# Attention weights sent through DRAM: each softmax row stored twice, copied from there to the partitions of its head, and the output projections spread over the step

## The chip, the cores and the metric

The kernel runs on one NeuronCore of one Trainium2 chip. It is one program that holds four layers one after the other, all in float32. The time is the device time of one execution in microseconds. The kernel before was timed three times: 10415.69 us is the median, 10412.58 the lowest and 10416.83 the highest. One further execution was recorded by the hardware profiler; it has its own time, given with its span below.

The engines are named as in the profile: PE is TensorE (matrix products), PEld its weight loads, DVE is VectorE, ACT is ScalarE, POOL is GpSimd, and SP is SyncE, which here only issues DMA transfers. Each engine runs its own instructions strictly in order and waits for others by semaphores.

## The reference, cut to what matters

The input x has 8 images, 16 channels, 128 x 128 points. Four layers are applied, each as x = x + layer(groupnorm(x)). Only the first one is touched in its inner loop:

```python
def layer0(in_x, w_attn, w_attn_proj, w_fc, w_fc_proj, conv_w, conv_b):
    # per point: the 3x3 neighbourhood, wrapped, as 3 tokens of 48 (a column of 3 rows x 16 channels)
    x = fold(in_x)                                  # [N, 3, 48],  N = 8*128*128
    h = ln(x)
    q, k, v = split(h @ w_attn.T)                   # 4 heads of 12
    att = softmax(einsum('nhtd,nhsd->nhts', q, k) / sqrt(12))      # 3 x 3 weights per head
    y = einsum('nhts,nhsd->nhtd', att, v)
    x = x + y @ w_attn_proj.T
    h = ln(x)
    x = x + gelu(h @ w_fc.T) @ w_fc_proj.T          # 48 -> 192 -> 48
    x = ln(x)
    return conv1x1(sum(x, axis=tokens)) + conv_b
```

The three tokens s of a query t are the left, middle and right neighbours, and since the weights add to one, y = v_middle + a_left (v_left - v_middle) + a_right (v_right - v_middle). Both kernels use this: they need only two of the three weights, and the differences dv of neighbouring v.

## The kernel before, in words

**Tiling.** Layer 0 (lines 242 to 786) goes over the image in 32 steps of 4 rows, that is 512 points of each image. A tile has 128 partitions: two images (g), each with 48 values of a token in a block of 64 partitions, and 512 points in the free dimension. Eight images make four such pairs k; d = 0, 1 counts couples of pairs, so that a tile of 128 x 1024 holds two pairs. PSUM has 8 banks of 512 columns, `banks`: bank 0 collects variances, bank 1 the attention scores, and the rest is handed out in pairs of banks by `two()`, in a ring.

**A software pipeline.** The loop at line 688 runs four stages of four successive steps side by side. `ahead` (two steps on) is loaded and centred (`load`, `center`); `then` (one step on) gets its first normalization, q, k, v, the products q*k (`multiply`), the scores (`scores`) and the softmax; `new` gets attention, projection, second normalization and the first four of its six MLP units; `old` gets the last two units (4 and 5), the variances for the last normalization, and the final sum; `done` is stored.

**Order.** Matrix products are emitted in the order of the program and held in it by `in_turn("pe", ...)` (lines 218 and 374). So the PE has one fixed list, and a product that waits for its input holds up all that follows it. The attention products on DVE and POOL are held in turn in the same manner. The lists of the other engines come from the program's order and the scheduler, and are in order too.

**The attention step before.** `softmax` (line 510) leaves normalized weights `att` on 96 partitions: row 32*u + 8*k + 4*g + h for the query u, the pair k, the image g and the head h. The values v have one partition per head element, so each weight row must be copied to the 12 partitions of its head. `attend(k, j, at)` (line 533) does this with three matrix products by a 0/1 matrix `spread` into three PSUM banks; DVE multiplies those with `dv` into `y` (line 543, 128 x 1536, one operand in PSUM), and POOL subtracts it from v or adds it (lines 551 and 553, 128 x 1536). There are 8 such calls in a step: four pairs k, and j = 0 (left), 2 (right). `project` (line 556) multiplies y by the projection `wpc`, and DVE adds the result to the centred input (line 565).

**Where they stand.** The part that follows the softmax is a list of 8 slots, `between` (lines 696 to 741). Each slot begins with one `attend` and then has pieces of other work: units 4 and 5 of `old` in slots 0 to 5, back projections and projections 0,0 to 0,2 in slots 6 and 7, and then `qkv` of the next step. Projections 1,0 to 1,2 stand behind the slots, line 744.

**Queues.** SP issues the loads of `xin` (24 a step), the load and store of the finished rows (lines 619 and 627) and, in step 0, the small weights of layer 1 (line 734). ACT issues the other constants at the start. In layer 1, ACT issues the loads `bs` (line 845) ahead of its square root.

Of the kernel before, what the change touches and what calls it, by code (L numbers as in the profile page):

```python
# [9 lines left out]
F32 = mybir.dt.float32  # L10
AF = mybir.ActivationFunctionType
ALU = mybir.AluOpType
# [24 lines left out]
def _constants():  # L37
# [20 lines left out]
    score[token, 24 + 4 * g + h] = 1.0  # L58
    parts["score"] = score
    spread = np.zeros((128, 4, 128))  # L60
    bcast = np.zeros((128, 5, 128))
    last = np.zeros((128, 2, 2, 32))
    for t in range(4):
        bcast[32 * t + 16 + g, 4, token] = 1.0
        for n in range(4):
            bcast[32 * t + 4 * (n // 2) + 2 * (n % 2) + g, n, token] = 1.0
            spread[32 * t + 8 * n + 4 * g + h, n, token] = 1.0
# [3 lines left out]
    parts["spread"] = spread.reshape(128, 512)  # L71
# [34 lines left out]
def kernel(  # L106
# [29 lines left out]
    from_ = _WHERE["pair"][1]  # L136
    const = cpool.tile([128, _CONST.shape[1] - from_], F32, name="const")
    nc.scalar.dma_start(const, const_in[:, from_:])

    def k_(name):  # L140
        n, lo, hi = _WHERE[name]
        return const[:n, lo - from_ : hi - from_]
# [83 lines left out]
    w1s, b1s = [], []  # L226
    for n in range(5):
        t = cpool.tile([BC, BC], F32, name=f"w1_{n}")
        nc.gpsimd.memset(t, 0.0)
        for b in range(B):  # L230
            r = slice(b * C, (b + 1) * C)
            loads.append((t[r, r], w1[n].rearrange("i o -> o i") if n < 2 else w1[n]))
        w1s.append(t)
        b1s.append(rep(b1[n], B, f"b1_{n}"))
# [7 lines left out]
    with ExitStack() as l0:  # L242
# [19 lines left out]
        def k0(name):  # L262
# [4 lines left out]
        spread, bcast = (  # L267
            k0(name).rearrange("p (n m) -> p n m", m=128) for name in ("spread", "bcast")
        )
# [27 lines left out]
        for i in range(3):  # L297
            for g in range(2):
                r = slice(64 * g + i * 16, 64 * g + i * 16 + 16)
                nc.scalar.dma_start(  # L300
                    wqkv[r, :, :E], w0_qkv[i].rearrange("c (n o) -> c n o", n=3)
                )
# [13 lines left out]
        for g in range(2):  # L316
            nc.scalar.dma_start(wpc[64 * g : 64 * g + E, :E], w0_proj)
# [39 lines left out]
        def work(name):  # L357
            return tmp.tile([128, 2, 512], F32, tag="work", name=name, bufs=11)

        def large(name):  # L360
            return tmp.tile([128, 3, 512], F32, tag="large", name=name, bufs=5)
# [56 lines left out]
        class Step:  # L418
# [23 lines left out]
            def center(self, d):  # L442
                p = two()
                blocks(p, lambda k: wcen[:, 2 * d + k], xin[:, 2 * d : 2 * d + 2])
                self.xc[d] = act.tile([128, 2, 512], F32, name="xc", bufs=5)
# [17 lines left out]
            def qkv(self, d):  # L463
                q = self.q[d] = work("q")
# [19 lines left out]
            def multiply(self, d, engine):  # L484

                for k in range(2):
                    parts = []
                    for at, n in ((0, 3), (3, 2)):
                        t = large("pd")
                        ins = (nc.vector if engine == "dve" else nc.gpsimd).tensor_mul(  # L490
                            t[:, :n].rearrange("p n (a b) -> p n a b", a=4),
# [18 lines left out]
            def softmax(self):  # L510

                a = self.att = act.tile([96, 3, 512], F32, name="att")
# [1036 lines left out]
```

## Time and profile before

| what | value |
|---|---|
| median of 3 runs | 10415.69 us |
| time of the profiled execution | 10417.28 us |
| its span, first to last instruction | 10415.5 us |
| layer 0, from the span's start | about 0 to 3192 us |
| one steady step of layer 0 | 94.45 us (the same product starts at 1509.06 and 1603.51 us) |
| busy in 1000 to 2000 us | PE 913, DVE 507, ACT 548, POOL 639 us |
| DMA share in the same stretch | 6% of 16 engines, 15 GB/s |

Busy shares are averages over the four layers; layers 2 and 3 take the time after about 3320 us and are bound by other engines than layer 0. What a change in layer 0 is worth is read from one steady step: which engine works without a gap, and what ends its gaps. In timeline rows the columns are start (us), length (us), engine, line, operation, what is written and read, and in brackets the idle time before it and what ended it. A product in float32 shows as two matmul records. The granted clock of TensorE (PEclk) is a share of full speed.

### The profile page before, as it was taken

Reading aid. Unit: us, or ns where it says so; the run is one execution under the profiler, and the core shown is the slowest. Engines: PE = TensorE matmul, PEld = TensorE weight load, DVE = VectorE, ACT = ScalarE, POOL = GpSimd, SP = SyncE. Lnnn points to the kernel's source line nnn. Section 1 sums busy time; section 2 is a strip of 40 time slices with the busy share of each in tenths; the row PEclk is TensorE's granted clock in tenths of the full one; section 3 lists DMA queues with packets and bytes.
Section 4 is the critical chain, followed back from the end, with each engine's and each line's share of the span. In section 5 each row is a group of like instructions: output and inputs, shape, how many; then the busy total and the mean of one; then the engine's idle time right before and its main releaser. Section 6 shows DMA issues by size and latency. Waiting matters only on the chain.

```text
span 10415.5 us, 192029 instructions
## 1 busy us (share of the span) xinstructions
PE 8808.0 (85%) x81400; PEld 2482.8 (24%) x81400; DVE 8490.1 (82%) x6774; ACT 8595.5 (83%) x7107; POOL 5545.7 (53%) x2608
## 2 busy tenths in 40 slices
PE   6999999999996888888888888888888888888799
PEld 1222222222222222222222222222222222222222
DVE  4545554554555999999999999999999999999977
ACT  3555555555555999999999999999999999999988
POOL 4666666666652555555555555555555555555421
PEclk8999999999998999999999999999999999999999
DMA  1000000000002000000000000000000000000022
GB/s 53 13 15 15 14 14 15 15 13 15 15 7 77 14 21 16 18 21 14 21 14 21 14 20 21 14 21 14 21 14 21 17 18 20 14 13 9 14 62 62
DMA packets 203668, 215.74 MB, mean 21 GB/s; under 512 B 50616, under 2 KB 159416, under 8 KB 200760
## 3 DMA queue, kind: packets, MB, share of 16 engines
q1 hardware_dynamic: 197544, 198.27, 7.0%
q8 instruction: 640, 10.49, 0.4%
q10 hardware_dynamic: 5264, 5.17, 0.2%
q14 instruction: 220, 1.80, 0.1%
HBM read 117.80 MB, written 60.04 MB: 17 GB/s over the span
## 4 chain that ended last, share of the span: by engine, by line
DVE 43%; PE 25%; issue 21%; ACT 8%; DMA 2%; SPq 1%; POOL 0%; DVEq 0%; ACTq 0%; POOLq 0%
PE banks L375 18%; DVE u L1078 15%; DVE pn L1078 10%; DVE u L1082 9%; DVE t L1068 2%; PE pn L1019 2%; PE pd L1019 2%; PE acc L1398 2%; DVE y L543 2%; DVE x L565 1%; ACT hid L157 1%; ACT sq L571 1%; ACT u L157 1%; DMA f<-yd 1%; DVE x L662 1%
## 5 line engine op out<-in xcount | busy, mean ns | idle before, releaser
L1091 POOL TENSOR_TENSOR v<-t,u 128x1280 f32<-128x1280 f32 x1152 | 3449.8, 2995 | 3080.8 <-DVE t L1068 3044.7
L1068 DVE SCALAR_TENSOR_TENSOR t<-t,u 128x2048 f32<-128x2048 f32 x1152 | 2632.7, 2285 | 32.3 <-ACT u L157 31.2
L1019 PE MATMUL pd<-f,wb 32*64 32x512 f32 x18432 | 2510.2, 608 | 92.8 <-ACT t L1057 40.5
L1057 ACT ACTIVATE t<-pd 128x1024 f32<-128x1024 f32 x2304 | 2364.9, 1026 | 133.2 <-PE pd L1019 75.0
L1019 PE MATMUL pn<-f,wa 32*64 32x512 f32 x18432 | 1299.4, 615 | 1112.1 <-DVE u L1082 1111.9
L157 ACT ACTIVATE u<-u 128x2048 f32<-128x2048 f32 x1152 | 2208.9, 1917 | 0.0
L157 ACT ACTIVATE u<-t 128x2048 f32<-128x2048 f32 x1152 | 2204.0, 1913 | 0.0
L1078 DVE TENSOR_TENSOR u<-pn,u 128x1280 f32<-128x1280 f32 x1152 | 1718.8, 1492 | 122.2 <-DVE pn L1078 2.8
L157 ACT ACTIVATE hid<-banks 128x1024 f32<-128x1024 f32 x576 | 569.9, 1023 | 1049.6 <-PE banks L375 1048.3
L1110 PE MATMUL acc<-u,const 128*32 128x512 f32 (+2 forms) x13824 | 1112.1, 454 | 0.0
L1078 DVE TENSOR_TENSOR pn<-pn,u 128x768 f32<-128x768 f32 x1152 | 1103.3, 958 | 0.0
L1082 DVE SCALAR_TENSOR_TENSOR u<-t,pn 128x768 f32<-128x768 f32 x1152 | 1087.6, 944 | 0.0
L1019 PEld LDWEIGHTS pd<-f,wb 32*64 32x64 f32 x18432 | 615.1, 130 | 1249.6 <-ACT t L1057 891.8
L1019 PEld LDWEIGHTS pn<-f,wa 32*64 32x64 f32 x18432 | 275.7, 130 | 2117.2 <-DVE u L1082 2109.7
L1110 PE MATMUL acc<-v,const 128*32 128x512 f32 (+1 forms) x9216 | 763.2, 449 | 1.5 <-POOL v L1091 1.5
L490 POOL TENSOR_TENSOR pd<-q,kp 128x1536 f32<-128x1536 f32 x248 | 674.6, 2732 | 11.2 <-PE banks L375 9.1
L571 ACT ACTIVATE sq<-x 128x1024 f32<-128x1024 f32 x384 | 395.3, 1053 | 272.6 <-DVE x L565 172.8
L375 PE MATMUL banks<-h,wfc 64*128 64x512 f32 (+1 forms) x3072 | 598.5, 617 | 14.6 <-DVE h L638 14.6
L638 DVE TENSOR_TENSOR h<-banks,x 128x1024 f32<-128x1024 f32 x192 | 232.6, 1211 | 428.2 <-PE banks L375 219.2
L543 DVE TENSOR_TENSOR y<-banks,dv 128x1536 f32<-128x1536 f32 x256 | 448.2, 1751 | 140.4 <-PE banks L375 134.1
L1110 PEld LDWEIGHTS acc<-u,const 128*32 128x32 f32 x13824 | 366.6, 109 | 812.6 <-issue 812.6
L553 POOL TENSOR_TENSOR y<-y 128x1536 f32<-128x1536 f32 x128 | 442.1, 3454 | 197.8 <-DVE y L543 197.5
(198 smaller groups left out, 8370.6 us busy)
## 6 DMA issues: line engine op xcount, KB each, us to landing
f<-yd SPq DMA_DIRECT2D x1016, 60.9 KB
yd<-y SPq DMA_DIRECT2D x280, 130.0 KB
xin<-in_x SPq DMA_DIRECT2D x744, 32.0 KB
four<-sil SPq DMA_DIRECT2D x256, 65.0 KB
xj<-in_x SPq DMA_DIRECT2D x8, 1024.0 KB
s<-in_x SPq DMA_DIRECT2D x32, 256.0 KB
x1d<-s SPq DMA_DIRECT2D x32, 256.0 KB
x<-x1d SPq DMA_DIRECT2D x8, 1024.0 KB
```

Source lines behind the costliest of these rows:

```text
L157: ins = nc.scalar.activation(out_, in_, func, **kw).ins
L375: in_turn("pe", mm(*args, skip_group_check=True, **kw).ins)
L490: ins = (nc.vector if engine == "dve" else nc.gpsimd).tensor_mul(t[:, :n].rearrange("p n (a b) -> p n a b", a=4), rows(self.q[d][:, k]).un ...
L543: ins = nc.vector.tensor_mul(out_, banks[:, at : at + 3].rearrange("p n (a b) -> p n a b", a=4), windows(dv, j // 2, 3),).ins
L571: nc.scalar.activation(self.sq[d][u], self.x2[d][:, u], AF.Square)
L1019: yield mm(p[64 * (u % 2) : 64 * (u % 2) + 64, u // 2], w[lo : lo + 32, q % 2, n].rearrange("p c f -> p (c f)"), fs[k * NP + q][lo : lo + ...
L1057: in_turn("act", nc.scalar.activation(self.t[:, ab], self.pd, AF.Abs).ins)
L1068: ins = nc.vector.scalar_tensor_tensor(self.t, self.t, 1.0, self.u, op0=ALU.add, op1=ALU.mult).ins
L1078: in_turn("dve", nc.vector.tensor_mul(u if cols.start else p, p, u).ins)
L1082: ins = nc.vector.scalar_tensor_tensor(u, t, 2.0, p, op0=ALU.subtract, op1=ALU.mult).ins
L1091: ins = nc.gpsimd.tensor_mul(self.v, t, u).ins
L1110: ins = mm(accs[k][32 * q : 32 * q + 32, lo % 512 : (hi - 1) % 512 + 1], gather[:, int(part == 1), g], flat(c.u)[:, ab, lo:hi] if src is N ...
```

## The change

The weights no longer go through TensorE. After the softmax, SP stores the two wanted weights of all 96 rows to a DRAM tile `shared`, each row twice (768 KB). For each query u and each pair k, SP then copies 8 rows, 16 with their doubles, from DRAM into the tile `y` on 128 partitions, each of the 16 read 8 times (512 KB): a head now has 16 partitions instead of 12. DVE multiplies `y` with `dv` in place (two operands in SBUF, 128 x 1024), subtracts the two halves (128 x 512), and POOL adds v (128 x 512). The unit is one query of one couple, (d, u), six in a step with two pairs each. `attend` stands in slots 0 to 5 and the projection of the same (d, u) two slots later, in slots 2 to 7.

The layout of q, k, v and `wpc` is padded to 16 per head; the tiles stay 64 wide. The weight tile is reordered to left, right, middle. The pool `work` has 9 buffers instead of 11, `xc` 4 instead of 5, `y` has 4 of its own, and the products `pd` have 3 + 2. The finished rows reuse the tile `z`, and their load and store move to slots 6 and 7. Some centring, scaling and variance work moves by a slot or within slot 7. To make room, most of the constants and the weights of layer 1 are loaded when layer 0 is over, on ACT's queue.

```diff
+    score[64 * g + 16 * h + r % HD, 24 + 4 * g + h] = 1.0
-            spread[32 * t + 8 * n + 4 * g + h, n, token] = 1.0
...
-    w1s, b1s = [], []
-    for n in range(5):
-        t = cpool.tile([BC, BC], F32, name=f"w1_{n}")
-        nc.gpsimd.memset(t, 0.0)
-        for b in range(B):
-            r = slice(b * C, (b + 1) * C)
-            loads.append((t[r, r], w1[n].rearrange("i o -> o i") if n < 2 else w1[n]))
-        w1s.append(t)
-        b1s.append(rep(b1[n], B, f"b1_{n}"))
+    b1s = [rep(b1[n], B, f"b1_{n}") for n in range(5)]
...
-                nc.scalar.dma_start(
-                    wqkv[r, :, :E], w0_qkv[i].rearrange("c (n o) -> c n o", n=3)
-                )
+                for n in range(3):
+                    nc.scalar.dma_start(
+                        wqkv[r, n].rearrange("c (h d) -> c h d", h=NH)[:, :, :HD],
+                        w0_qkv[i][:, n * E : (n + 1) * E].rearrange("c (h d) -> c h d", h=NH),
+                    )
...
-            nc.scalar.dma_start(wpc[64 * g : 64 * g + E, :E], w0_proj)
+            for h in range(NH):
+                lo = 64 * g + 16 * h
+                nc.scalar.dma_start(wpc[lo : lo + HD, :E], w0_proj[h * HD : (h + 1) * HD])
...
-            return tmp.tile([128, 2, 512], F32, tag="work", name=name, bufs=11)
+            return tmp.tile([128, 2, 512], F32, tag="work", name=name, bufs=9)
...
                 nc.vector.tensor_mul(
-                    a[:, 0::2], a[:, 0::2], sm.unsqueeze(1).to_broadcast([96, 2, 512])
+                    a[:, 0:2], a[:, 0:2], sm.unsqueeze(1).to_broadcast([96, 2, 512])
                 )
-            def attend(self, k, j, at):
-
-                for u in range(3):
-                    r = slice(32 * u, 32 * u + 32)
-                    pe(banks[:, at + u], spread[r, k], self.att[r, j], start=True, stop=True)
-                y = large("y")
-                v, dv = (
-                    t[k // 2][:, 4 * (k % 2) : 4 * (k % 2) + 4] for t in (self.v, self.dv)
+                self.shared = dram.tile([96, 2, 1024], F32, name="shared", bufs=2)
+                weights = a[:, 0:2].rearrange("p n m -> p (n m)")
+                nc.sync.dma_start(
+                    self.shared, weights.unsqueeze(1).to_broadcast([96, 2, 1024])
                 )
-                out_ = y.rearrange("p n (a b) -> p n a b", a=4)
-                ins = nc.vector.tensor_mul(
-                    out_,
-                    banks[:, at : at + 3].rearrange("p n (a b) -> p n a b", a=4),
-                    windows(dv, j // 2, 3),
-                ).ins
-                in_turn("dve", ins)
-                if j == 0:
-                    self.y[k] = y
-                    ins = nc.gpsimd.tensor_sub(out_, windows(v, 1, 3), out_).ins
-                else:
-                    ins = nc.gpsimd.tensor_add(self.y[k], self.y[k], y).ins
-                in_turn("pool", ins)
+            def attend(self, d, u):
+
+                for k in (2 * d, 2 * d + 1):
+                    y = tmp.tile([128, 2, 512], F32, name="y", bufs=4)
+                    lo = 32 * u + 8 * k
+                    nc.sync.dma_start(
+                        y.rearrange("p n m -> p (n m)"),
+                        self.shared[lo : lo + 8]
+                        .rearrange("h n m -> (h n) m")
+                        .unsqueeze(1)
+                        .to_broadcast([16, 8, 1024]),
+                    )
+                    v, dv = (t[d][:, 4 * (k % 2) : 4 * (k % 2) + 4] for t in (self.v, self.dv))
+                    out_ = y.rearrange("p n (a b) -> p n a b", a=4)
+                    in_turn("dve", nc.vector.tensor_mul(out_, out_, windows(dv, u, 2)).ins)
+                    in_turn("dve", nc.vector.tensor_sub(y[:, 0], y[:, 1], y[:, 0]).ins)
+                    at = rows(y[:, 0])
+                    ins = nc.gpsimd.tensor_add(at, at, v[:, :, u + 1 : u + 1 + W]).ins
+                    in_turn("pool", ins)
+                    self.y[k, u] = y
...
             if done:
-                put(2, done.store)
-            if new:
-                put(6, new.project, 0, 0)
-                put(6, new.project, 0, 1)
-                put(7, new.project, 0, 2)
-                put(7, new.square, 0)
+                put(6, done.store)
+                put(7, done.write)
             if ahead:
-                put(7, ahead.center, 0)
+                put(6, ahead.center, 0)
             if then:
-                put(7, then.scaled, 0)
+                put(6, then.scaled, 0)
...
             for i, fs in enumerate(between):
-                if new:
-
-                    new.attend(i // 2, i % 2 * 2, 4 if not old and i < 7 and i % 2 else 1)
+                if new and i > 1:
+                    new.project(*divmod(i - 2, 3))
+                if new and i < 6:
+                    new.attend(*divmod(i, 3))
                 for f in fs:
                     f()
-            ring["from"] = 1
-            if new:
-                for u in range(3):
-                    new.project(1, u)
-                new.square(1)
...
+        w1s = []
+        for n in range(5):
+            t = wp.tile([BC, BC], F32, name=f"w1_{n}")
+            nc.gpsimd.memset(t, 0.0)
+            for b in range(B):
+                r = slice(b * C, (b + 1) * C)
+                nc.scalar.dma_start(t[r, r], w1[n].rearrange("i o -> o i") if n < 2 else w1[n])
+            w1s.append(t)
```

## The prediction, written before the changed kernel was timed

> **What bounds the kernel now.** I read the page's busy line first, then stretches of layer 0, then the groups by line, and last the timelines of PE, DVE and POOL over one steady step. Page and stretch:
>
> ```profile
> PE 8808.0 (85%) x81400; PEld 2482.8 (24%) x81400; DVE 8490.1 (82%) x6774; ACT 8595.5 (83%) x7107; POOL 5545.7 (53%) x2608
> ...
> 1000.00:2000.00 1000.00, 913.23 (x5536) 252.19 (x5530) 506.81 (x414) 547.91 (x576) 639.14 (x360) 0.98 0.06 15
> ```
>
> Columns of the second line: stretch, length, busy PE, PEld, DVE, ACT, POOL, granted clock, DMA share, GB/s. In layer 0 PE is 91% busy, the rest at most 64%, and DMA idles. PE's fixed list bounds it. What the change takes from that list, and PE's rows in one step:
>
> ```profile
> L375 PE MATMUL banks<-att,const 32*128 32x512 f32 x486 | 105.3, 646 | 28.9 <-DVE y L543 15.8 <-DVE att L529 13.1
> ...
> 1544.09 1.04 PE L375 MATMUL banks<-h,wfc 64*64 64x512 f32 x8
> ...
> 1547.25 1.14 PE L375 MATMUL banks<-att,const 32*128 32x512 f32 x6 [2.13 <-DVE att L529]
> ...
> 1583.55 1.95 PE L375 MATMUL banks<-hn,wqkv 64*64 64x512 f32 x16
> ...
> 1591.30 2.81 PE L375 MATMUL banks<-y,wpc 64*64 64x512 f32 x24
> ```
>
> Call t = 0 the end of the first of these four, 1545.13: PE is through unit 3 and waits 2.1 us for the softmax. At t = 38.4 qkv of the next step starts. Between lie slots 0 to 7.
>
> **The change, part by part.**
>
> *PE.* 24 products (48 records) leave each step: in the PE timeline a group of three takes 1.07, so 8 x 1.07 = 8.6 us. Projections 1,0 to 1,2 move ahead of qkv (2.8 us), which only re-orders. To compare alike, qkv "before" starts at 38.4 + 2.8 = 41.2. PE's idle time in that stretch is 5.8 us by the brackets; without it and the 8.6, 27 us of work remain. The gain is bounded by 8.6 + 5.8 = 14.4 us a step, if y were always ready.
>
> *The path to y.* It was: product, DVE, POOL. It becomes: store to DRAM, load, DVE twice, POOL. Prices:
>
> ```profile
> 1545.99 1.21 DVE L529 TENSOR_TENSOR att<-att,mx 96x1024 f32<-96x1024 f32 x1
> ...
> 1530.27 0.69 DVE L520 TENSOR_TENSOR mx<-mx,att 96x512 f32<-96x512 f32 x1
> ...
> 1542.75 1.18 POOL L614 TENSOR_TENSOR s<-s,z 128x512 f32<-128x512 f32 x1
> ...
> SPq L794 <- DMA x1d<-s: 3.2, 1, 3.2
> ...
> 3195.00:3200.00 5.00, 0.58 (x2) 0.50 (x2) 0.66 (x4) 1.47 (x2) 0.00 (x0) 0.50 1.02 321
> ```
>
> A multiply on SBUF operands is 1.2, a subtraction 0.7, a POOL add 1.2. The third group is SyncE's wait for a 256 KB store to DRAM, 3.2 us; at the 321 GB/s of a full queue (DMA share 1.02) its bytes are 0.8, which leaves 2.4 fixed. It stood behind 1 MB loads, so an idle queue should be quicker: I take 2.1, ends 1.0 and 2.4. Store, 768 KB: 2.1 + 2.4 = 4.5. Load, 512 KB: 2.1 + 1.5 (350 GB/s, between 301 and 419 of the neighbouring stretches) = 3.6, each further one 1.5.
>
> *DVE against POOL.* Before, the multiply read PSUM and one SBUF operand; now multiply and subtraction read two in SBUF, as one old line does in layer 1:
>
> ```profile
> 3229.74 3.48 DVE L820 TENSOR_TENSOR wa<-dense,const 128x64 f32<-128x64 f32 x9
> ...
> 3229.96 2.36 POOL L933 TENSOR_TENSOR y<-y,gate 128x1024 f32<-128x1024 f32 x1 [1.22 <-DVE gate L929]
> ...
> 3241.86 1.30 DVE L820 TENSOR_TENSOR wa<-dense,const 128x64 f32<-128x64 f32 x9
> ...
> 3242.08 3.29 POOL L933 TENSOR_TENSOR y<-y,gate 128x1024 f32<-128x1024 f32 x1 [2.00 <-DVE gate L929]
> ```
>
> Nine small ones take 1.30, but 3.48 when POOL's 2.36 us began within them: they waited out its whole length. In the other pair POOL pays, 3.29 for 2.36. So a POOL add and a DVE operation on two SBUF operands exclude each other, and I count them as one resource. The Trainium skill (SBUF — State Buffer, "Who interferes with whom") says the same and speaks against this change: a DVE instruction with two SBUF inputs contends with a GpSimd instruction that reads SBUF, and the loser blocks for the whole instruction; if they only shared bandwidth, the walk below would come out about 5 us a step shorter.
>
> *The order on DVE,* from the built program: multiply and subtract pair 0, multiply pair 1, then the DVE add of the previous projection (L565, 1.2; in slots 0 and 4 the add after a back projection), then subtract pair 1. So the subtraction waits for the previous projection, behind which PE waits for POOL. A load needs one of four y tiles, so that of slot i + 2 waits for projection i.
>
> *The walk* (us after t = 0). Weights ready 2.1, stored 6.6, y landed 10.2, 11.7, 13.2, 14.7. Slot 0: multiply to 11.4, subtract to 12.1, second multiply to 13.3 (POOL shut out), POOL add and the 1.2 of L662 side by side to 14.5, subtract to 15.2, slot 1's multiply to 16.4, POOL add to 17.6; projection 0,0 ends at 18.9. Slot 1: subtract 18.4, multiply 19.6, projection's add 20.8 beside POOL's, subtract 21.5, POOL 22.8; projection 0,1 ends at 24.0. Slot 2 cannot start before its load (18.9 + 3.6 = 22.5). In the same way the others end at 31.4, 36.5, 45.1, 51.2, some 6.5 a slot. Four records of variances (1.9) follow, so qkv starts at 53.0 against 41.2: **+11.8 us a step**, and PE idles for half of the stretch.
>
> Bounds. Below: first y at 8.2 (1.0 fixed), no exclusion: DVE must do 12 x 1.2 + 12 x 0.7 + 7 x 1.2 = 31.2 in order, then 1.2 + 1.1, and 1.9: qkv at 43.9, +2.7. A gain is excluded unless DVE's rows are shorter than any here. Above: loads at half the rate (16 rows read 8 times each; no row shows it) add 1.5 a slot: +21.
>
> *PE's clock.* The gap before projection 0,0 is some 11 us.
>
> ```profile
> 182.82 1.94 PE L375 MATMUL banks<-hid,wfp 128*64 128x512 f32 x8 [0.40 <-ACT hid L157]
> ...
> 192.97 3.68 PE L375 MATMUL banks<-hid,wfp 128*64 128x512 f32 x8 [3.36 <-ACT hid L157]
> ...
> 110.00:120.00 10.00, 9.51 (x33) 2.55 (x30) 9.00 (x6) 0.00 (x0) 9.10 (x3) 0.50 0.03 1
> ```
>
> After 3.4 us idle the same products take 3.68 for 1.94; in step 0, after 14.6 idle, the clock stays at 0.50 for over 10 us of sparse work. Projections 0,0 to 0,2 at half speed add 1 each to the path: +3 (ends 0 and 8). The Trainium skill (TensorE: Matmul & The Clock Gate, "What's actually happening") has the clock back after about 3.4 us of sustained work; by that rule only the burst after the first gap is slow, about 1 instead of 3. The walk gave POOL the worse of most ties; I take 2 off for the even case. **+13 a step.**
>
> *Steps.* 32 with attention: 32 x 13 = 416. Step 0 has no units 4 and 5 to fill PE: 8 more (0 to 20).
>
> *SP.* 13 more issues a step. Those of `xin` (16.5 us in all) and of the finished row come behind the blocked loads, but are needed a step later: nothing, while the step is some 50 us longer than their wait. The 40 issues removed in step 0 were on an idle queue.
>
> *Start.* ACT issues 18 more weight loads at 0.57: 10.3, of which 6 were idle time before its square root: +5 (0 to 10).
>
> *Layer 1.*
>
> ```profile
> L734 SPq DMA_DIRECT2D w<-in_w x40: 417/418/447, 81.1 to 114.4; - x40
> ...
> 3186.92 11.57 ACTq L845 DMA_DIRECT2D bs<-in_w_base  x8
> ...
> 3199.81 0.20 ACT L157 ACTIVATE s<-var 128x1 f32<-128x1 f32 x1
> ```
>
> 41 issues now stand on ACT between the end of layer 0 and that square root, with DVE's reciprocal, the scaled weights and PE's first product behind it. At 0.42 they take 17; queued like `bs` (1.45 each) far more, but with small transfers: +20 (12 to 30).
>
> *Pools.* Fewer work and xc tiles: the sixth square or next xc may wait for a PE or DVE read that is then past: 0 (up to 1 a step). POOL's busy time falls (26 to 14 us in y), but its q*k products start with kp, as before: no gain.
>
> **Sum.** 416 + 8 + 5 + 20 = 449 on the profiled 10417.28, which is 1.6 above the median of 10415.69: 10,865 on the median.
>
> **Rivals.**
> 1. *Milder (+5 a step).* DMA near its lower end, few lock conflicts, clock kept: 160 + 33, 10,610. For: the bound of +2.7; POOL is often ready in DVE's waits. Against: the L820 rows.
> 2. *Harsher (+20).* Loads slow, or half clock through the stretch: 640 + 33, 11,090. For: the 0.50 row. Against: PE works in bursts over 3 us from slot 3 on.
> 3. *Faster.* y is hidden and PE keeps 12 of the 14.4: 10,417 - 384 + 33 = 10,066. It decides if projection 1,2 ends by t = 39.4. Against: DVE's 31.2 alone, after the first landing at 8.2.
> 4. *Nothing moves.* Tail savings (3 us idle behind qkv) cancel the bound of +2.7.
>
> **How the numbers follow.** Forecast 0.58 (its own range 10,700 to 11,000), rival 1 0.21, rival 2 0.15, rival 3 0.04, rival 4 0.02. So slower by over 0.2%, about what a measurement here can tell, 0.94; faster 0.04; same 0.02. The range leaves out rivals 3 and 4 and the tails: 10,570 to 11,110.
>
> **What would show it.** Right: PE busy in layer 0 near 75%, step near 107 us, largest PE wait before the products of y, released by POOL L550, 8 us or more in slot 0; y multiplies or POOL adds up to twice 1.2; half-speed projections; ACT's square root in layer 1 some 20 us later. Wrong if the first load lands before t = 8, if multiplies and adds overlap at full length, or if projection 1,2 ends near 40.

## The result, and the profile after

The changed kernel takes 10791.28 us (median, 10780.60 to 10798.71) against 10415.35 for the kernel before: 1.036 times as long, with a 95% interval of 1.0343 to 1.0378. Its profiled execution took 10798.71 us, with a span of 10796.9, 381.4 longer than the span before.

The page's line of the engines, and the same stretch of layer 0 as shown of before (columns: stretch, length, busy PE, PEld, DVE, ACT, POOL, granted clock, DMA share, GB/s):

```profile
PE 8744.4 (81%) x79864; PEld 2440.2 (23%) x79864; DVE 8861.8 (82%) x7286; ACT 8568.6 (79%) x7107; POOL 5391.4 (50%) x2736
...
1000.00:2000.00 1000.00, 818.34 (x4556) 215.83 (x4551) 560.30 (x519) 488.23 (x523) 529.90 (x362) 0.92 0.31 77
```

PE falls from 913 to 818 us of a thousand and no engine takes its place: nothing in layer 0 is busy all the time any more. That is the mark of a chain that goes round several engines. The costliest groups of the y path in the page (busy us, mean ns | idle before and its releaser):

```profile
L550 POOL TENSOR_TENSOR y<-y,vp 128x512 f32<-128x512 f32 x384 | 684.8, 1783 | 948.2 <-DVE y L548 925.1
...
L369 PE MATMUL banks<-y,wpc 64*64 64x512 f32 x1536 | 487.9, 768 | 505.7 <-POOL y L550 500.5
...
L547 DVE TENSOR_TENSOR y<-y,dv 128x1024 f32<-128x1024 f32 x384 | 498.5, 1298 | 214.3 <-DMA y<-shared 212.4
```

PE waits 500 us for POOL, POOL 925 for DVE, DVE 212 for the loads. POOL's addition takes 1.78 us on average, where the shortest takes 1.09.

One step's front in the timeline of all engines, where t = 0 (the end of unit 3's last wfc product) is 1595.19:

```profile
1596.06 1.21 DVE L524 TENSOR_TENSOR att<-att,mx 96x1024 f32<-96x1024 f32 x1
...
1597.29 0.57 SPq L529 DMA_DIRECT2D shared<-att  x1
...
1602.04 10.34 SPq L538 DMA_DIRECT2D y<-shared  x5
...
1606.64 1.22 DVE L547 TENSOR_TENSOR y<-y,dv 128x1024 f32<-128x1024 f32 x1 [4.68 <-DMA y<-shared]
...
1608.92 1.92 DVE L547 TENSOR_TENSOR y<-y,dv 128x1024 f32<-128x1024 f32 x1 [0.33 <-DMA y<-shared]
...
1609.82 1.97 PE L369 MATMUL banks<-y,wpc 64*64 64x512 f32 x4 [6.29 <-POOL y L550]
...
1614.71 1.12 PE L369 MATMUL banks<-y,wpc 64*64 64x512 f32 x2 [2.93 <-POOL y L550]
```

The weights are ready at t = 2.1, the store's end releases the first load at 6.85, the first y is there at 11.4, the second 2.3 later, and the first product of y starts at 14.6, at half clock (1.97 for four records that take 1.08 at full clock, as the run with idle products below shows).

Means over all steady steps (27 to 30 a kernel, from the DVE and PE timelines between 200 and 3400 us; times in us after the end of the softmax's last multiply, which is t = 2.1):

| kernel | first y multiply | last subtraction ends | last y product ends | qkv starts | from there to the next softmax's end | whole step |
|---|---|---|---|---|---|---|
| before | 2.0 | - | behind qkv | 37.8 | 58.2 | 95.98 |
| changed | 9.3 | 45.7 | 50.0 | 51.9 | 54.7 | 106.57 |

With the 2.8 us of moved projections, qkv before counts as 40.6: the stretch grew by 11.3 and the rest shrank by 0.7.

Where the 381.4 us of span came from, each from the rows of the same instruction in both traces:

| stretch | before | after | difference |
|---|---|---|---|
| start to the first softmax's last multiply | 106.8 | 103.2 | -3.6 |
| from there to that of the 32nd softmax, 31 steps | 2975.2 | 3309.2 | +334.0 |
| from there to layer 0's last norm (L415, now L409) | 102.2 | 124.3 | +22.1 |
| from there to layer 1's first gate product | 29.2 | 60.2 | +31.0 |
| the rest | 7202.1 | 7200.0 | -2.1 |

The fourth row holds two things. Layer 1's start, in ACT's timeline, and one row of DVE's:

```profile
3539.90 30.89 ACTq L807 DMA_DIRECT2D w<-in_w  x40
3571.70 13.32 ACTq L851 DMA_DIRECT2D bs<-in_w_base  x8
...
3586.34 0.20 ACT L160 ACTIVATE s<-var 128x1 f32<-128x1 f32 x1
```

```profile
3550.00 0.75 DVE L617 SCALAR_TENSOR_TENSOR z<-z,bias 128x512 f32<-128x512 f32 x1 [9.48 <-DMA z<-in_x]
```

ACT's square root waits behind 40 + 8 issues: from the variance to the first gate product 41.9 us pass, before 17.2 (+24.7). And DVE waits 9.5 us for the x rows of the last finished step (+6.3 from the norm to the end of those rows): their load now goes into `z`, which POOL must have left first, and nothing follows that could hide it.

### The profile page after: what moved, and what is told of

Its sections match the earlier page's. It is cut to its first block, busy times and chain, and to the rows that moved or that the text cites. A ratio compares the mean times of both kernels' runs of the same rounds, so it can differ in the third digit from the quotient of the medians.

```text
span 10796.9 us, 190835 instructions
## 1 busy us (share of the span) xinstructions
PE 8744.4 (81%) x79864; PEld 2440.2 (23%) x79864; DVE 8861.8 (82%) x7286; ACT 8568.6 (79%) x7107; POOL 5391.4 (50%) x2736
## 4 chain that ended last, share of the span: by engine, by line
DVE 43%; issue 23%; PE 20%; DMA 6%; ACT 5%; POOL 2%; SPq 1%; DVEq 0%; ACTq 0%; POOLq 0%
PE banks L369 15%; DVE u L1084 15%; DVE pn L1084 10%; DVE u L1088 9%; DMA y<-shared 3%; DVE t L1074 2%; POOL y L550 2%; PE pn L1025 2%; DMA shared<-att 1%; DVE y L547 1%; PE pd L1025 1%; DVE y L548 1%; PE acc L1404 1%; DMA f<-yd 1%; ACT att L366 1%
## 5 line engine op out<-in xcount | busy, mean ns | idle before, releaser
L1063 ACT ACTIVATE t<-pd 128x1024 f32<-128x1024 f32 x2304 | 2359.1, 1024 | 130.5 <-PE pd L1025 67.9
L550 POOL TENSOR_TENSOR y<-y,vp 128x512 f32<-128x512 f32 x384 | 684.8, 1783 | 948.2 <-DVE y L548 925.1
L369 PE MATMUL banks<-y,wpc 64*64 64x512 f32 x1536 | 487.9, 768 | 505.7 <-POOL y L550 500.5
L369 PE MATMUL banks<-h,wfc 64*128 64x512 f32 (+1 forms) x3072 | 724.2, 665 | 69.8 <-DVE h L638 38.3
L547 DVE TENSOR_TENSOR y<-y,dv 128x1024 f32<-128x1024 f32 x384 | 498.5, 1298 | 214.3 <-DMA y<-shared 212.4
```

The source lines that it names most:

```text
L369: in_turn("pe", mm(*args, skip_group_check=True, **kw).ins)
L547: in_turn("dve", nc.vector.tensor_mul(out_, out_, windows(dv, u, 2)).ins)
L550: ins = nc.gpsimd.tensor_add(at, at, v[:, :, u + 1 : u + 1 + W]).ins
L1063: in_turn("act", nc.scalar.activation(self.t[:, ab], self.pd, AF.Abs).ins)
```

## The experiments

Theory after the result: the loss is the prediction's chain, a round trip through DRAM at the front and DVE and POOL shutting each other out behind it. Rivals: the four y buffers (loads that wait for projections), PE's clock, PE's own order.

In the table that sums them up, steps are means as above; the runs with six y buffers start 8 to 9 us later (first softmax at 111.3 to 112.6 instead of 103.2), so steps compare better than medians there.

| run | median | ratio to before, 95% | step |
|---|---|---|---|
| changed kernel | 10791.28 | 1.0343 to 1.0378 | 106.57 |
| slot 0 by PE | 10736.41 | 1.0289 to 1.0320 | 105.13 |
| v on PE (no POOL in y) | 10720.18 | 1.0279 to 1.0313 | 104.58 |
| six y buffers | 10729.90 | 1.0286 to 1.0317 | 104.36 |
| slot 0 by PE + v on PE | 10732.70 | 1.0284 to 1.0318 | 105.16 |
| v on PE + six buffers | 10645.81 | 1.0205 to 1.0239 | 101.85 |
| all three | 10595.95 | 1.0163 to 1.0193 | 100.73 |
| kernel before | 10415 | | 95.98 |

### Weights of the step before

```diff
-                self.shared = dram.tile([96, 2, 1024], F32, name="shared", bufs=2)
-                nc.sync.dma_start(self.shared, weights...)          # in softmax
+                if new and i == (0 if new.source is None else 2):   # in slot 2
+                    new.keep()                                      # the store
-                        self.shared[lo : lo + 8]
+                        self.source[lo : lo + 8]                    # stored a step earlier
```

> The loads of a step read the weights that the step before had stored (so y, and with it the attention, is computed from the wrong rows); the store is still made, behind the first loads. Nothing waits for the round trip through DRAM any more. Theory (the round trip opens the gap, the DVE-POOL chain of some 6 us a slot follows it): the first multiply starts near t = 3 instead of 11.4, the chain behind it keeps its length, qkv starts some 8 us earlier, and the clock is not lost in the gap: -8 to -10 us a step, 10,480 to 10,530 us. Rival (the DVE-POOL chain and its lock alone set the time, the round trip only shifts it under other work): under 3 us a step, above 10,690.

Measured: 11073.22, ratio 1.0617 to 1.0649: 282 us slower than the changed kernel. Neither theory. With nothing to wait for, the order of DVE's instructions, which is fixed when the kernel is built, came out otherwise: the multiplies and subtractions of slots 0 and 1 stand ahead of the norm's two operations (L407, L409) of the step before, in the stretch where POOL makes q times k. The timeline there:

```profile
1561.14 2.37 POOL L484 TENSOR_TENSOR pd<-q,kp 128x1024 f32<-128x1024 f32 x1
...
1561.24 3.35 DVE L552 TENSOR_TENSOR y<-y,dv 128x1024 f32<-128x1024 f32 x1 [8.41 <-POOL dv L476]
...
1565.25 1.21 DVE L552 TENSOR_TENSOR y<-y,dv 128x1024 f32<-128x1024 f32 x1
...
1579.05 2.07 PE L369 MATMUL banks<-rstd,const 32*128 32x512 f32 x4 [16.86 <-DVE rstd L409]
```

A multiply of 1.21 takes 3.35 when POOL's 2.37 began 0.1 us earlier: it waits out that one's whole length. PE then stands 16.9 us for the norm. The run says nothing on the round trip, but shows the lock at its plainest, and that where the y operations stand on DVE matters more than when their data come.

### The same with the order of the changed kernel

```diff
+                self.source = steps.get("stale", self.shared)
+                steps["stale"] = self.shared
-                        self.shared[lo : lo + 8]
+                        self.source[lo : lo + 8]
```

> The loads of a step read the buffer that the step before had stored, issued right behind this step's store, in the place and order of the changed kernel (y is computed from the wrong rows). Only the wait for the store's arrival is gone, 4.7 us by SyncE's rows; the loads now share the DMA with the store's 768 KB (about 2.4 us of it). Theory (the chain from the first landing to the last projection is paced by DVE, so that the front moves it one to one): the first multiply 2.3 to 4.7 us earlier and the step as much shorter, 10,640 to 10,720 us. Rival (something later in the stretch, the four buffers or the banks, sets the end): under 1 us a step, above 10,760.

Measured: 11090.16 (1.0630 to 1.0662). The order was not kept: the first loads moved ahead of the store, and slots 0 and 1 ahead of the norm, as in the run above (step 116.2 against 116.1). The price of the round trip by itself stays unmeasured; what follows takes it away in another manner.

### v on PE

```diff
+                        v = self.v[d][r : r + 64, 4 * k : 4 * k + 4, u + 1 : u + 1 + W]
+                        pe(p[o : o + 64, k], wpc[r : r + 64], v, start=True, stop=False)
-                        pe(p[o : o + 64, k], wpc[r : r + 64], y, start=True, stop=True)
+                        pe(p[o : o + 64, k], wpc[r : r + 64], y, start=False, stop=True)
-                    ins = nc.gpsimd.tensor_add(at, at, v[:, :, u + 1 : u + 1 + W]).ins
-                    in_turn("pool", ins)
```

> POOL's addition of v is left out; PE adds wpc times v itself, four more products of 0.27 us to a projection, ahead of those of y; the function computed is the reference's. This takes POOL out of the chain, and with it both its own stage and the lock. Theory (DVE and POOL exclude each other): a slot goes from some 6.1 us to 2 x (1.2 + 0.7) + 1.2 = 5.0, qkv starts 6 to 8 us earlier, 10,540 to 10,600. Rival (loads and their four buffers set the pace of the slots, POOL only adds its last 2 us): -2 us a step, near 10,730.

Measured: 10720.18, 71 us less than the changed kernel. The rival's size, but not its cause: the last subtraction ends at 41.1 after the softmax and not 45.7, as the theory had it, while the last y product ends at 48.6 and not 50.0. Rows of the timeline at the end of one stretch (the softmax's multiply ends at 1461.77):

```profile
1501.96 0.69 DVE L548 TENSOR_TENSOR y<-y 128x512 f32<-128x512 f32 x1
...
1503.96 1.21 DVE L565 TENSOR_TENSOR x<-banks,xc 128x1024 f32<-128x1024 f32 x1
...
1505.22 1.42 PE L369 MATMUL banks<-rstd,const 32*128 32x512 f32 x4 [2.42 <-DVE x L565]
...
1506.94 1.98 PE L369 MATMUL banks<-vp,wpc 64*64 64x512 f32 x8 [0.30 <-DVE x L664]
...
1508.70 1.35 PE L369 MATMUL banks<-y,wpc 64*64 64x512 f32 x8
```

y is ready at 1502.65, its product comes 6 us later: PE's list first has products that need a pair of PSUM banks each, which DVE frees by additions that now stand behind its y operations. Of the 6 us PE waits 2.7 for these additions; the rest goes to the products ahead, among them those of v (1.98), which this edit adds. DVE gained 4.6 us a step, and the new wait and PE's new work took back all but 1.4 of it at the last product (2.0 over the step).

### v on PE, POOL beside it

```diff
+                    ins = nc.gpsimd.tensor_add(
+                        rows(y[:, 1]), rows(y[:, 0]), v[:, :, u + 1 : u + 1 + W]
+                    ).ins
+                    in_turn("pool", ins)
```

> As the run with v on PE, but POOL still makes all its 12 additions, into the half of the tile that nobody reads: PE does not wait for them, so only the lock with DVE is left of POOL. Against the run with v on PE: if a POOL addition and a DVE operation on two SBUF operands exclude each other, 12 x 1.1 us less what lies beside DVE's additions from PSUM (7 x 1.2): +3 to +6 us a step, 100 to 190 us slower than that run; if they merely share bandwidth or POOL yields, under 1 us a step, at most 30 us slower.

Measured: 10865.95 (1.0419 to 1.0451), 146 us more than the run without POOL, or 4.6 a step, though no product waits for what POOL computes; the last subtraction is back at 45.7. DVE's groups in 1000 to 2000 us, of the run without POOL and then of this one:

```profile
L547 DVE TENSOR_TENSOR y<-y,dv 128x1024 f32<-128x1024 f32 x111 | 135.5, 1221 | 61.7 <-DMA y<-shared 61.6
L548 DVE TENSOR_TENSOR y<-y 128x512 f32<-128x512 f32 x110 | 75.7, 688 | 2.5
```

```profile
L547 DVE TENSOR_TENSOR y<-y,dv 128x1024 f32<-128x1024 f32 x114 | 144.6, 1268 | 48.0 <-DMA y<-shared 47.8
L548 DVE TENSOR_TENSOR y<-y 128x512 f32<-128x512 f32 x114 | 126.6, 1111 | 2.6
```

The subtraction goes from 0.69 to 1.11 us, the multiply from 1.22 to 1.27. A load into the same buffer has to wait for POOL's addition too, but that is not the cause: DVE's wait for loads fell, from 61.6 to 47.8 us. The lock is shown, with its price. That this run is slower than the changed kernel itself fits: it has the lock, and the waits and products of v on PE besides (the last y product ends 7.9 us behind the last subtraction here, 7.6 with v on PE alone, 4.3 in the changed kernel).

### Keeping PE's clock

```diff
+                for i in range(20 if (d, u) == (0, 0) else 0):
+                    r, k = 64 * (i % 2), i // 2 % 2
+                    pe(p[r ^ (64 * k) : ...], wpc[r : r + 64], v, start=True, stop=True)
```

> 20 idle products (5.4 us at full clock, of wpc and v, into the bank that projection 0,0 then overwrites) stand on PE ahead of projection 0,0, in the gap of 6.3 us. If the clock is kept by them, projections 0,0 to 0,2 run at 1.07 us for four products and not 1.97; the prediction's term for the clock was 3 us a step, so -2 to -3 us a step, 10,695 to 10,730. Rival: DVE paces the slots and takes up what PE gains, under 0.5 us a step, 10,775 to 10,810; or the half clock comes in spite of the products, and nothing changes in the projections.

Measured: 10818.40 (1.0373 to 1.0404), no gain, rather a loss (step 107.3 against 106.6). PE's timeline, and two stretches of it (same columns as above; the granted clock is the third number from the end):

```profile
1514.06 4.49 PE L369 MATMUL banks<-vp,wpc 64*64 64x512 f32 x40
1520.43 1.08 PE L369 MATMUL banks<-y,wpc 64*64 64x512 f32 x4 [1.88 <-POOL y L550]
...
1525.33 1.12 PE L369 MATMUL banks<-y,wpc 64*64 64x512 f32 x2 [3.82 <-POOL y L550]
```

```profile
1517.00:1521.00 4.00, 2.12 (x20) 0.50 (x12) 3.42 (x3) 0.00 (x0) 1.09 (x1) 1.00 1.03 230
1525.00:1529.00 4.00, 3.67 (x16) 1.06 (x16) 3.96 (x4) 0.00 (x0) 2.75 (x3) 0.50 0.10 23
```

Projection 0,0 starts at full clock, 1.08 and not 1.97, and PE merely waits longer for the next y, 3.82 and not 2.93. So full clock for its first pair gains nothing, as the rival has it. But the idle products kept the clock for that pair alone: while PE waits it falls again, and the second pair and projection 0,1 run at 0.50 as in the changed kernel. What the half clock costs in projections 0,0 to 0,2 together, this run does not show. Why it is 27 us slower was not traced.

### w1 on POOL's queue

```diff
-                nc.scalar.dma_start(t[r, r], w1[n].rearrange("i o -> o i") if n < 2 else w1[n])
+                nc.gpsimd.dma_start(t[r, r], w1[n].rearrange("i o -> o i") if n < 2 else w1[n])
```

> One word: the 40 loads of w1 ahead of layer 1 are issued by POOL instead of ACT. In the profile of the changed kernel ACT's square root stands 31.3 us behind the variance it needs, with 30.9 us of these issues and 13.3 of bs ahead of it; before, 3.6 behind it. If the issues hold it, it comes 15 to 25 us earlier: 10,766 to 10,776. Rival (the transfers themselves, or bs, hold it; or POOL issues more slowly and the scaled weights wait for it): under 5 us, above 10,786.

Measured: 10771.53 (1.0326 to 1.0357). The two intervals overlap, so the median's 20 us need the trace: from the last norm to the first gate product 43.2 us instead of 60.2. ACT's timeline:

```profile
3539.34 11.58 ACTq L851 DMA_DIRECT2D bs<-in_w_base  x8
...
3558.15 0.20 ACT L160 ACTIVATE s<-var 128x1 f32<-128x1 f32 x1 [5.92 <-DVE var L205]
```

The square root now waits for its variance alone (3557.96) and comes 0.2 us behind it, in the changed kernel 31.3. So the issues held it. Of this 17.0 us reach the gate product: the last row's load lands 3.4 later, and DVE waits 6.3 us for w1 itself and then 5.4 for a memset that stands behind POOL's issues.

### Slot 0 by PE

```diff
+    spread[8 * n + 4 * g + h, n, 64 * g + 16 * h + r % HD] = 1.0
+                    if (d, u) == (0, 0):
+                        w = two()
+                        for j in range(2):
+                            pe(w[:, j], spread[0:32, k], self.att[0:32, j], start=True, stop=True)
+                    else: ...                                        # the load, as it was
+                ins = nc.vector.tensor_mul(self.h2, p, self.x2[d][:, u]).ins
+                if i == 5:
+                    in_turn("dve", ins)                              # keeps unit 5's multiply early
```

> Slot 0's two y tiles (projection 0,0) get their weights as before the change, by two products each into PSUM (4 of 0.36 us a step), the other ten from DRAM; the function is the reference's. DVE begins y about 3.6 us after t = 0 and not 11.4, and has slot 0 and the norm's multiply done when the first load lands. Theory (front and DVE chain add up): -5 to -6.5 us a step, 10,580 to 10,630 us. Rival (the first slot was hidden by the DVE's two other operations or the loads pace the rest): -2 us or less, above 10,720.

Measured: 10736.41, 55 us less, a good quarter of what the theory said. DVE starts y at 3.1 after the softmax and not 9.3, and its last subtraction ends at 45.4 and not 45.7. Rows of the timeline of one step (softmax's end at 1579.02):

```profile
1579.07 7.11 PE L373 MATMUL banks<-att,const 32*128 32x512 f32 x8 [2.13 <-DVE att L528]
...
1582.80 1.22 DVE L558 TENSOR_TENSOR y<-banks,dv 128x1024 f32<-128x1024 f32 x1 [2.65 <-PE banks L373]
...
1593.48 1.04 PE L373 MATMUL banks<-y,wpc 64*64 64x512 f32 x8
...
1599.36 1.23 DVE L558 TENSOR_TENSOR y<-y,dv 128x1024 f32<-128x1024 f32 x1 [1.45 <-DMA y<-shared]
```

Slot 0's four products take 7.1 us of PE here, 6.2 on average between 500 and 3300 us, and not 4 x 0.36. They all read the same 32 partitions, and their eight records follow one another, mostly at half clock; before, the three of a group read 32 partitions each of their own, start together and take 1.14. So what stands behind them on PE comes later. Slot 2's load waits for projection 0,0 to free its buffer. That projection has its y at 1589.33, but stands in PE's list behind pieces of unit 4 and ends at 1594.52; 4.8 us later slot 2's multiply starts, 20.3 after the softmax, where the changed kernel starts it at 21.3. Six us were won at the front, and PE's new work and the buffers took back five. The run does not tell these two apart, so its 55 us are no clean price of the round trip.

### Six y buffers

```diff
-        xin = wp.tile([128, NP, 512], F32, name="xin")
+        xin = wp.tile([128, 2, 512], F32, name="xin")
-                self.dv[d] = act.tile([128, 8, W + 4], F32, name="dv", bufs=2)
+                self.dv[d] = act.tile([128, 8, W + 4], F32, name="dv", bufs=1)
-                    v, dv = (t[d][...] for t in (self.v, self.dv))
+                    v, dv = (t[d][...] for t in (self.v, self.v))
-                    y = tmp.tile([128, 2, 512], F32, name="y", bufs=4)
+                    y = tmp.tile([128, 2, 512], F32, name="y", bufs=6)
```

> Six y buffers and not four. There is no room for them in SBUF, so the kernel computes on wrong data: xin holds two images for four (same number and size of loads), and the multiplies read v in the place of dv (same shapes; dv is still made). A load then waits for the projection of three slots back, not two. In the changed kernel DVE waits once more for a load after the front, 2.7 us in slot 4. Theory (the buffers are a third limit, just behind DVE and POOL): -0.5 to -1.5 us a step, 10,740 to 10,775. Rival (they set the pace): -3 us or more, under 10,700.

Measured: 10729.90; step -2.2. Between the two theories: more than a limit just behind, less than the one that sets the pace.

### Pairs, and all three

The three edits together, and two of their pairs; the diffs are those above.

> Slot 0 by PE and v on PE together, nothing else; the function is the reference's. The first alone gave 55 us, the second 71. If front and POOL's part are two terms of one sum: about 126 less than the changed kernel, 10,665. If both run into the same next limit (four y buffers: in the run with all edits DVE waited 2 to 3.6 us for loads in slots 2 and 4): little more than the better of them, 10,700 to 10,725. If each had hidden the other: under 10,620.

> v on PE and six y buffers (on the wrong data of that run), but slot 0 from DRAM as in the changed kernel. Without the first slot by PE, DVE starts y at t = 11.4 again. Alone v on PE gave 71 us and six buffers 61; all three edits 195. If the front counts one to one once nothing else limits: 3 to 6 us a step more than with all three, 10,700 to 10,790, so no gain at all from the pair is its worst case. If POOL and the buffers are the pair that hid each other and the front is filled by other work of DVE and PE: within 60 us of all three, 10,600 to 10,655.

> The run before with six y buffers (on the wrong data of the run with six buffers). If the buffers are what front and POOL ran into: 31 us of DVE's work from t = 6 with no wait, the last projection near t = 41, -7 to -10 us a step against the changed kernel, 10,470 to 10,570. If PE's order and its PSUM banks hold it instead (a product of v takes its bank long before y is there, and the banks wait for DVE's additions): within 30 us of the run with four buffers.

Measured: slot 0 and v on PE together 10732.70, 59 us, no more than v on PE alone and nearest to the second alternative (the same next limit). v on PE and six buffers 10645.81, 145 us, a little over the sum of 71 and 61, in the range given for POOL and the buffers hiding each other. All three 10595.95, 195 us, somewhat short of what was expected of it. With four buffers slot 0 by PE adds nothing to v on PE, with six it adds 50 us. So the front and POOL together do run into the buffers. (Slot 0 by PE with six buffers and POOL still in y was not run.) That the multiplies read v, which is ready before dv, is not what the six buffers gain by: in the changed kernel 212.4 of the 214.3 us that DVE waits ahead of these multiplies are for loads. DVE's group of the multiplies that wait for loads, in 500 to 3300 us, of slot 0 and v on PE (five of six slots), then of all three:

```profile
L558 DVE TENSOR_TENSOR y<-y,dv 128x1024 f32<-128x1024 f32 x270 | 329.4, 1220 | 149.4 <-DMA y<-shared 148.9
```

```profile
L558 DVE TENSOR_TENSOR y<-y,vp 128x1024 f32<-128x1024 f32 x280 | 341.1, 1218 | 59.7 <-DMA y<-shared 59.7
```

With four buffers DVE waits 148.9 us in 27 steps, 5.5 a step, though slot 0 needs no load; with six, 2.1.

### All edits that keep the function

The edits of slot 0, v on PE and w1 on POOL's queue, and:

```diff
-                put(6, then.scaled, 0)
+                put(4, then.scaled, 0)
-                put(7, then.qkv, 0)
+                put(6, then.qkv, 0)
-                put(6, done.store)
+                put(7, done.store)
```

> Slot 0 by PE, v on PE (POOL out of y), the 40 loads on POOL, and the norm's scaling and qkv 0 of the next step moved ahead of projections 1,1 and 1,2, where PE waits; the row's store behind them. If front (5 to 6.5), lock and POOL stage (2 to 8) and the late qkv (3) add up: -10 to -14 us a step, 93 to 97 against 95.97 before, 10,350 to 10,460 us: about the kernel before, perhaps under it. Rival (the next chain, q times k on POOL, which starts with qkv, takes the gain back): 100 us a step or more, above 10,540.

Measured: 10789.32 (1.0323 to 1.0365), no better than the changed kernel, worse than slot 0 and v on PE alone. qkv 0 does start at 43.1 after the softmax, but from there to the next softmax's end it is 64.8 instead of 54.7, and the step is 108.0: the last y product ends at 52.8, qkv 1 follows it, and the scores need both. None of the kernels tried is faster than the kernel before, and the one that comes nearest lacks the room in SBUF to be a real one.

## Why the prediction was right, and where it was not

It said 10,865 (10,570 to 11,110) and slower; it is 10,791. By its own steps:

- **Bound.** Right: PE was the bound, lost its 8.6 us of products, and idles now (913 to 818 us of a thousand; 75% busy was foretold, it is 82, as products at half clock take about twice as long).
- **The walk.** qkv 11.8 us later, it said; 11.3 on average. Inside it two sizes were off: the first y is there at 11.4 and not 10.2, since the load takes 4.6 and not 3.6, and further loads follow each other by 2.3 and not 1.5. The store's 4.5 was 4.75. That the end fits all the same is in part luck. On average projection 0,0 ends at 21.5, where it said 18.9, and the last one at 52.1, where it said 51.2; qkv starts at 54.0 for its 53.0, and before at 42.7, where the one step that it read gave 41.2. And the walk adds the front and the slots one to one, which no run confirms. Its lower bound comes to 43.6 from the terms it gives, and not 43.9, which changes nothing.
- **The lock.** Without exclusion "about 5 us a step shorter", it said: 4.6 by the pair of runs with and without POOL's idle additions. That is what the Trainium skill states (SBUF — State Buffer, "Who interferes with whom": the loser blocks for the whole instruction), and the rows agree, 3.35 for 1.21 beside a POOL product of 2.37. But the walk let one cause carry it. Taking POOL out returned 2.0 us a step, taking slot 0's round trip out 1.4, both together 1.4. The buffers, which the walk named once ("that of slot i + 2 waits for projection i"), and the PSUM banks, which it did not name, stand right behind, and both edits also pay with products on PE.
- **The clock** is the term that no run confirms: "projections 0,0 to 0,2 at half speed add 1 each to the path: +3", less 2 for ties. They do run at half clock, but the walk without the term is already 0.5 over what was measured, and the one run on it raised the clock for the first pair of projection 0,0 alone, without a gain. DVE's additions behind the projections hardly wait for PE in the changed kernel, 6.6 us in 1000 to 2000 us, 0.7 a step; what half clock adds by way of the buffers was not measured. The Trainium skill (TensorE: Matmul & The Clock Gate, "What's actually happening") lets the clock return after some 3.4 us of sustained work. Here PE works in pieces between waits, and the granted clock is 0.50 for 20 us on end. And the row that the prediction read as "sparse work" does not agree with the rule: PE was busy for 9.51 of those 10 us, and the clock stayed at 0.50. What it takes to bring the clock back was not tested. The rows of the changed kernel:

```profile
1607.00:1627.00 20.00, 12.81 (x36) 3.19 (x40) 18.69 (x17) 5.38 (x6) 11.18 (x6) 0.50 0.67 166
...
L563 DVE TENSOR_TENSOR x<-banks,xc 128x1024 f32<-128x1024 f32 x56 | 68.1, 1216 | 6.6 <-PE banks L369 6.6
```

- **From qkv to the next softmax** it counted nothing; it is 0.7 shorter. With the clock's +1 and the 0.5 of the walk, neither of which came, this makes the step +10.6 and not +13: 77 us of the 31 steps, most of the miss. Their sum is 334, against 411.
- **Step 0**: 8 + 13 = 21 foretold, the first two softmaxes lie 112.5 instead of 92.1 apart: +20.4.
- **The last step** was not set apart: +22.1, where the walk has 13.
- **Start**: +5 foretold, -3.6 measured. ACT's first copies do come 1.7 later (18 more issues), but step 0's products are then faster: before, DVE waited 2.0 us there for a product buffer that three-wide and two-wide tiles shared. The rest of that gain was not traced.
- **Layer 1**: +20 (12 to 30) foretold, +24.7 measured; ACT's 40 issues took 30.9 and not 17, and those of `bs` 13.3.
- **The finished row**: "nothing, while the step is some 50 us longer than their wait". True of every step but the last, which has no next one: +6.3.

The rivals were not it: no gain on PE was kept (third), the step did not grow by only 5 us (first) nor by 20 (second), and did not stay as it was (fourth). The bounds were wide enough for the errors, which have both signs.

What stays open: with all three limits eased a step is still 4.8 us longer than before. There, PE's largest waits for another engine in 1000 to 2000 us are for DVE's additions that free PSUM banks:

```profile
PEld banks L373 <- DVE x L576: 83.0, 40, 4.7
...
PE banks L373 <- DVE x L576: 48.9, 29, 3.9
```

But PE is also as busy as before (913 us), since two of the three edits gave it work, v's products and those of slot 0. The same stretch of that run, and these two groups:

```profile
1000.00:2000.00 1000.00, 908.31 (x5317) 257.36 (x5316) 561.11 (x553) 507.00 (x545) 335.98 (x254) 0.92 0.30 73
...
L373 PE MATMUL banks<-vp,wpc 64*64 64x512 f32 x480 | 73.7, 687 | 37.3 <-DVE x L576 35.1 <-DVE x L677 2.2
...
L373 PE MATMUL banks<-att,const 32*128 32x512 f32 x73 | 55.8, 928 | 15.9 <-DVE att L528 15.9
```

That is 13 us a step, more than the 8.6 that the change had taken away. Whether the 4.8 are the wait for banks or PE's own work, no run tells: none changed the banks or the order of the additions. The round trip's own price was not isolated either, and the granted clock differs between the kernels of the table (0.92 to 0.95 in this stretch, 0.98 before), which no run held fixed.

## What to carry to other kernels

Work taken from the bounding engine can be worth nothing if it comes back as a chain round four engines: count the chain (here 11 us to the first input and 31 of DVE alone, in order) against the time that the old bound needed (41 us) before counting the savings. Where removing one limit gives little, ease the next ones with it, even in a kernel that reads v in the place of dv to make room: three edits of 55, 61 and 71 us gave 59 or 145 in pairs and 195 together, which showed the buffers behind the other two. Price the work that such an edit adds as well: slot 0's four products were taken for 1.4 us and cost PE 6.2. And an engine's additions beside a chain are not free if they share a lock with it, even when nobody waits for them.

## What the runs showed of the hardware that was not expected

- A load that reads 16 rows of 4 KB eight times each moves less than the queue's rate elsewhere: in the stretch below (same columns as above) the queue is full, at a share of 1.03, and moves 229 GB/s, where layer 1's loads before moved 321 at 1.02 (301 to 419 in the stretches beside). 512 KB at 229 GB/s are the 2.3 us between the first two landings. Whether the repeated reads or something else of these loads makes the difference was not tested.

```profile
1607.00:1612.00 5.00, 1.97 (x4) 0.29 (x4) 4.64 (x5) 0.00 (x0) 1.09 (x1) 0.50 1.03 229
1612.00:1617.00 5.00, 2.29 (x10) 0.77 (x12) 4.51 (x5) 0.00 (x0) 3.72 (x2) 0.50 0.47 121
```

- Most of the lock is paid by POOL: its additions are 1.78 us on average for 1.09 alone, DVE's subtraction 0.94 for 0.69, its multiply 1.30 for 1.22. The subtraction's group, and one case in the changed kernel's timeline: POOL's addition begins 0.15 after a multiply and takes 2.01; the subtraction behind the multiply then waits for it, 1.47.

```profile
L548 DVE TENSOR_TENSOR y<-y 128x512 f32<-128x512 f32 x384 | 359.5, 936 | 5.6
...
1612.50 1.21 DVE L547 TENSOR_TENSOR y<-y,dv 128x1024 f32<-128x1024 f32 x1
1612.65 2.01 POOL L550 TENSOR_TENSOR y<-y,vp 128x512 f32<-128x512 f32 x1 [2.89 <-DVE y L548]
1613.75 1.47 DVE L548 TENSOR_TENSOR y<-y 128x512 f32<-128x512 f32 x1
```

- Four products that read the same 32 partitions took 6.2 us on average, 3.7 at the shortest (slot 0 by PE), where three that read 32 partitions each of their own took 1.14 together in the kernel before.
